# Where GpSimd forms the sums of the output weights: two batches, or one behind the last convolution of the first group

## The chip, the cores and the metric

The kernel runs on one core of a Trainium2 chip. The core has five engines that run at the same time, each with its own queue of instructions: TensorE (PE in the profile, with PEld for its weight loads), VectorE (DVE), ScalarE (ACT), GpSimd (POOL) and SyncE (SP), which here issues nearly all DMAs. An engine works through its queue in order; an instruction that waits for another engine holds up everything behind it. The metric is the device time of one execution in microseconds; the median of the runs is compared.

## The reference

The input is x, 16 sequences of 256 tokens of 512 features, all in float32. Three layers follow each other, each with a residual and a layer norm.

```python
x = _layernorm(x + _L0_attn_ref(x, ...), axis=-1)      # a state-space layer
x = _layernorm(x + _L0_xattn_ref(x, k, skip, ctx, ctx, 8), axis=-1)   # a long convolution
x = _layernorm(x + _L0_ffn_ref(x, ...), axis=-1)       # a linear layer with routed LoRA
```

The change lies in the first:

```python
xn = x * rsqrt(mean(x * x) + EPS) * w_norm
proj = einsum('bld,td->blt', xn, W_in)                 # z, xi, dt, Bm, Cm
xi = silu(causal depthwise conv of 4 taps(xi))
dt = softplus(dt + dt_bias);  dA = exp(-dt * exp(A_log))
u = (dt * mean of xi over a head)[..., None] * Bm
h = dA_t[..., None] * h + u_t;  y_t = sum(h * C_t)     # scan over the tokens
y = einsum('blh,ih->bli', y, W_h2i) * silu(z)
out = einsum('bli,di->bld', y, W_out) + residual
```

## The kernel before

The first layer runs in eight groups of 512 tokens (two sequences); the loop over g is at line 526. The second and third layers follow in another loop over eight slices and aren't touched.

**Products with seven instead of eight parts.** The projections and, in all groups but the last, the output product are formed with Strassen's scheme in Winograd's form: a product of two 2x2 block matrices from seven block products. The blocks' sums and differences must be made beforehand. For tokens these are `token_sums` (lines 221 to 226); for the projections' weights `weight_sums` (228 to 234), once, on GpSimd; for the output weights `w_o` it is `w_o_sums` (290 to 302), also once, on GpSimd, in the first group. With `w_o[r, j]` the four blocks, each of four tiles of 128x256, it makes T3 = w11 - w01 (line 295), T1 = w01 - w00 (298, in the place of w01), T2 = w11 - T1 (300) and T4 = w10 - T2 (301), sixteen instructions in all. T1 and T3 are read by the output products of the first group (`out_product`, line 740), T2 and T4 likewise.

**The order inside a group.** The scheduler is off: each engine's queue has the order in which the code calls its instructions. A loop over i (line 623) goes through ten projections; in the first group these are x0, x1, z0, x2, z1, x3, b0, c1, z2, z3. Each turn issues the first four block products of projection i, then the last three of projection i-1 (`finish_products`), the first sums of i (lines 344 to 347) and the last sums of i-1 (`finish_sums`, 356 to 359). When i-1 is an x, `finish_sums` also issues the convolution of two tiles of channels, `mixed` (552 to 566): on VectorE one scaling (559, or on ScalarE 557) and three multiply-and-adds (561) a tile. `mixes` collects the last of each tile. So the turn i = 4 holds the convolutions of tiles 4 and 5, and i = 6 those of tiles 6 and 7, the last of the group.

The tail of the group then runs on VectorE: `stepped` (583), `states` with one product (587) and two scans (590) for each of two halves ht, in turns i = 7 (ht 0) and i = 8 (ht 1), and `outputs` (595), one product a half. In turn i = 9 TensorE sums these over the states into `yps` (639), and ScalarE copies them to `yT` (662). After the loop `spread_heads` (698) multiplies by W_h2i, `gated` (712) gates z with the result, `out_sums` (731) makes the sums of the gated z, and the output products (740) use them with the sums of `w_o`.

**What GpSimd has in its queue in the first group.** `later` (489) puts `weight_sums` of later projections behind a convolution: `wait_for` adds a wait to the first of them for the last multiply-and-add issued so far, `mixes[-1]`. In turn i = 4 these are the sums of z2 and z3. `w_o_sums` is a generator with two parts. Its first part (T3) is issued in turn i = 4, directly behind them; its second part (T1, T2, T4) in turn i = 8, behind `rms(xs_next)`, whose last step `rstd` (375) is a GpSimd instruction.

**The next group's norm.** In turn i = 8 the squares of the next tokens are summed on ScalarE (371), VectorE makes the mean `ms` (373), GpSimd raises it to -1/2 (`rstd`, 375), and SP writes the result to a row in DRAM (`to_dram`, 394). After the loop SP loads the next tokens into `xnT` (217), which waits until TensorE has read the old ones, and reads the row back, spread over all partitions, as `rt` (398). VectorE then scales `xnT` by it (`normed`, 404). From `xnT` TensorE forms the dt product (418), and GpSimd the token sums (222 to 226).

Of the kernel before, what the change touches and what calls it, by code (L numbers as in the profile page):

```python
# [10 lines left out]
ALU = mybir.AluOpType  # L11
# [60 lines left out]
def decoder_kernel(  # L72
# [95 lines left out]
    def wait_for(ins, other):  # L168
        tc.add_manual_dep(
            ins.ins,  # L170
            other.ins.name,
            mybir.DependencyInfo(
                mybir.DependencyClass.Sync, mybir.DependencyReason.DATA
            ),
            reason="order",
        )
# [4 lines left out]
    with ExitStack() as s1:  # L181
# [89 lines left out]
        w_o = {}  # L271
# [15 lines left out]
        for k, name in enumerate(("T3", "T2", "T4")):  # L287
            w_o[name] = parts[k * HC : (k + 1) * HC]

        def w_o_sums():  # L290

            sub = nc.gpsimd.tensor_tensor
            w_o["T1"] = w_o[0, 1]
            for c in range(HC):
                sub(w_o["T3"][c], w_o[1, 1][c], w_o[0, 1][c], ALU.subtract)
            yield
            for c in range(HC):
                sub(w_o["T1"][c], w_o[0, 1][c], w_o[0, 0][c], ALU.subtract)
            for c in range(HC):
                sub(w_o["T2"][c], w_o[1, 1][c], w_o["T1"][c], ALU.subtract)  # L300
                sub(w_o["T4"][c], w_o[1, 0][c], w_o["T2"][c], ALU.subtract)
            yield

        xis = [p1.tile([P, GB, S + 3], F32, name=f"xi{i}") for i in range(4)]
        for t in xis:
# [25 lines left out]
        def first_products(w, p, third):  # L331

            al, be = [
                ps_s.tile([P, 512], F32, tag="s", name="s") if third else bank() for _ in range(2)
            ]
            product(al[:, 0:S], w, p, A11, "11", start=True)
            product(be[:, 0:S], w, p, S1, "T1", start=True)
            product(al[:, S:], w, p, S2, "T2", stop=True)
            product(be[:, S:], w, p, S3, "T3", stop=True)
            return al, be  # L340

        def first_sums(al, be, to):
            u = p2.tile([P, S], F32, tag="u", name="u", bufs=3)
            nc.scalar.copy(u, al[:, 0:S])
            nc.vector.tensor_tensor(u, u, al[:, S:], ALU.add)
            nc.vector.tensor_tensor(to[3], u, be[:, S:], ALU.add)
            nc.vector.tensor_tensor(to[3], to[3], be[:, 0:S], ALU.add)
            return u
# [146 lines left out]
        def with_identity(w):  # L495

            for k, blk in enumerate(BLOCKS_OUT):
                own = w[:, k, blk * P : (blk + 1) * P]
                if blk in SWAPPED_OUT:
                    for a, b in ((0, HP), (HP, 0)):  # L500
                        half = own[:, a : a + HP]
                        nc.vector.tensor_tensor(half, half, ident[:, b : b + HP], ALU.add)
                else:
                    nc.vector.tensor_tensor(own, own, ident, ALU.add)

        def centred(w, cols):

            ps = ps_t.tile([P, 512], F32, tag="tr", name="mw")
            for kc in range(KD):
                nc.tensor.matmul(  # L510
                    ps[:, 0:cols], share, w[:, kc, :], start=(kc == 0), stop=(kc == KD - 1)
                )
            for kc in range(KD):
                nc.vector.tensor_tensor(w[:, kc, :], w[:, kc, :], ps[:, 0:cols], ALU.subtract)
# [11 lines left out]
        for g in range(NG):  # L526
# [6 lines left out]
            accs, mixes, zs, zpairs, silus = [], [], [], [], []  # L533

            def places(kind, p):

                if kind == "x":
                    two = [t[:, :, 3:] for t in (xis[2 * p % 4], xis[2 * p % 4 + 1])]
                    return [t[:, b, :] for t in two for b in range(GB)]
                if kind == "z":  # L540
                    pair = gp.tile([P, 2, GT], F32, tag="zs", name="zs")
                    zpairs.append(pair)
                    two = [pair[:, e, :] for e in range(2)]
                    zs.extend(two)
                else:
                    two = [p2.tile([P, GT], F32, tag=kind, name=kind) for _ in range(2)]
                    (Bs if kind == "b" else Cs).extend(two)
                return [t[:, b * S : (b + 1) * S] for t in two for b in range(GB)]
# [19 lines left out]
            def head_means(ht):  # L568

                xm = ps_t.tile([P, GT], F32, tag="tr", name="xm")  # L570
                for q in range(4):
                    nc.tensor.matmul(  # L572
                        xm[32 * q : 32 * (q + 1), :],
                        mean.rearrange("p h n -> p (h n)"),
                        accs[4 * ht + q].rearrange("p b s -> p (b s)"),
                        start=True,
                        stop=True,
                    )
                return xm

            def stepped(xm, dtS):
                m = p2.tile([P, GT], F32, tag="acc", name="m", bufs=6)
                nc.vector.tensor_tensor(m, xm, dtS, ALU.mult)
                return m
# [19 lines left out]
            def finish_products():  # L604
                kind, p, al, be, u, to = before
                last_products(al, be, kinds[kind], p)
# [16 lines left out]
            for i, (kind, p) in enumerate(order):  # L623
                if g == 1 and i == 2:
                    with_identity(w_f)
                if g == 1 and i in (5, 6):
                    centred(*((w_f, D), (w_gl, NE + ER))[i - 5])
                if i == 6:
                    ms = [head_means(0)]
                al, be = first_products(kinds[kind], p, i % 3 == 0)  # L630
                if i == 8:
                    ms.append(head_means(1))
                if i == 9:


                    yps = ps_t.tile([P, S], F32, tag="tr", name="yps")
                    for ht in range(HT):
                        for b in range(GB):
                            nc.tensor.matmul(
                                yps[b * HP : (b + 1) * HP],  # L640
                                sel[:, ht].rearrange("p q h -> p (q h)"),
                                Bs[ht][:, b * S : (b + 1) * S],
                                start=(ht == 0),
                                stop=(ht == HT - 1),
                            )
                if before is not None:
                    finish_products()
                to = places(kind, p)
                u = first_sums(al, be, to)
                if i == 8:  # L650
                    states(1, stepped(ms[1], spreads[2]), spreads[3])
                if i == 6:
                    ms = [stepped(ms[0], spreads[0])]
                    spreads.append(spread(1, 1))
                if g == 0:
                    if i == 1:
                        parts = decays()
                    if i in (1, 2, 4):
                        next(parts)
                if i == 9:  # L660
                    yT = q3.tile([P, S], F32, tag="vn", name="yT", bufs=1)
                    nc.scalar.copy(yT, yps)
                if before is not None:
                    finish_sums((lambda: next(parts)) if g == 0 and i == 2 else None)
                if g == 0 and i == 3:
                    next(parts)
                if g == 0 and i in later:
                    for n, (w, k) in enumerate(later[i]):
                        ins = weight_sums(nc.gpsimd, w, k)
                        if n == 0:  # L670
                            wait_for(ins, mixes[-1])
                    if i == 4:
                        w_sums = w_o_sums()
                        next(w_sums)
                if i == 7:
                    states(0, ms[0], spreads[1])
                if i == 8:
                    outputs(0)
                    outputs(1)
                    if more:  # L680
                        rt = to_dram(rms(xs_next))
                    if g == 0:
                        next(w_sums)
                before = (kind, p, al, be, u, to)
                if i < 2 and late:
                    normalised(g - 1, late.pop(0))
                if i == 1 and more:
                    xs_next = load_x(g + 1)
# [180 lines left out]
    with ExitStack() as s2:  # L869
# [295 lines left out]
        for h in range(HX):  # L1165
# [38 lines left out]
            behind = None  # L1204
            if nxt:
                kv_n, T_n = kvs[0]
                cT_n, vT_next = cTs[0], vT_after
                behind = products(vT_next, cT_n, kv_n, 0)
# [196 lines left out]
```

## Time and profile before

| | us |
|---|---|
| median of three runs | 1437.86 |
| lowest and highest | 1437.38, 1440.82 |
| the profiled execution | 1436.66 |
| its span in the profile | 1434.8 |
| TensorE busy in the span | 1417.2 |
| VectorE busy | 1218.1 |
| GpSimd busy | 560.8 |

The lines of the profile read as follows. A line of a timeline gives the start and the length in us, the engine, the line of the code and the operation, the tile written and the tiles read, the shapes, and how many instructions are merged. What stands in brackets at its end is the time that the engine stood idle before it and what ended that. A line of the list of waits gives the engine and line that waited, what it waited for, the sum in us, how often, and the longest. The mean granted clock of TensorE over the span is 0.998.

### The profile page before, as it was taken

To read this page: it belongs to the slowest core of one execution; us is meant where nothing else is said; L and a number is where in the kernel's file an instruction comes from. 1 tells how busy PE (TensorE), PEld (TensorE's weight loads), DVE (VectorE), ACT (ScalarE), POOL (GpSimd) and SP (SyncE) were. 2 spreads that over 40 slices of the span, in tenths; PEclk is the share of its full clock that TensorE was granted. 3 is DMA by queue.
4 is the path that set the end of the run, shared out by engine and by line. 5 is a ranking of instruction groups with operands and counts; after the bars stand their busy time and mean duration, and the time that the engine had idled before them with its cause. 6 is when DMAs were issued, how large, how long until landed. Compare 5 with 4: busy or idle time off the path is not lost.

```text
span 1434.8 us, 19174 instructions
## 1 busy us (share of the span) xinstructions
PE 1417.2 (99%) x6972; PEld 916.4 (64%) x6972; DVE 1218.1 (85%) x2101; ACT 461.9 (32%) x964; POOL 560.8 (39%) x654
## 2 busy tenths in 40 slices
PE   9999999999999999999998999999999999999997
PEld 7878788888888888888884444444444444444443
DVE  6988778778888787877848999999999999999996
ACT  2422323233232332332311433333333343333331
POOL 5540010110100201001004776777677667766772
PEclk9999999999999999999999999999999999999999
DMA  8014021120121101212003122212221222122200
GB/s 299 33 37 131 8 72 56 38 83 8 44 77 45 62 29 38 83 43 89 16 16 115 55 67 80 75 61 69 74 81 61 69 74 82 59 70 74 81 29 23
DMA packets 50815, 93.38 MB, mean 65 GB/s; under 512 B 10656, under 2 KB 15008, under 8 KB 50720
## 3 DMA queue, kind: packets, MB, share of 16 engines
q1 hardware_dynamic: 50192, 92.15, 20.1%
q8 instruction: 55, 0.90, 0.3%
q14 instruction: 40, 0.33, 0.1%
q10 hardware_dynamic: 528, 0.00, 0.0%
HBM read 74.82 MB, written 17.32 MB: 64 GB/s over the span
## 4 chain that ended last, share of the span: by engine, by line
PE 93%; DVE 5%; issue 1%; ACT 1%; DMA 0%; POOL 0%; SPq 0%; POOLq 0%; DVEq 0%; ACTq 0%
PE mm L322 18%; PE y L981 15%; PE s L322 13%; PE y L999 12%; PE base L1160 8%; PE s L740 6%; PE mm L740 6%; PE yc L969 4%; PE gl L1227 2%; PE base L1156 2%; PE tr L1071 1%; DVE acc L561 1%; PE mm L698 1%; PE xm L572 1%; PE mm L827 1%
## 5 line engine op out<-in xcount | busy, mean ns | idle before, releaser
L1034 DVE TENSOR_TENSOR pr<-y,cT 128x1024 f32<-128x1024 f32 x126 | 148.4, 1220 | 41.6 <-PE y L999 37.2
L158 DVE TENSOR_TENSOR kv<-vT,cT 128x1024 f32<-128x1024 f32 x128 | 180.1, 1448 | 1.5 <-ACT vT L148 1.5
L999 PE MATMUL y<-kv 64*64 64x512 f32 x1408 | 179.6, 598 | 0.0
L561 DVE SCALAR_TENSOR_TENSOR acc<-xi,wc,acc 128x512 f32<-128x512 f32 x192 | 143.5, 761 | 7.4 <-ACT acc L557 1.8
L1044 DVE TENSOR_REDUCE red<-pr 128x128 f32<-128x1024 f32 x126 | 147.1, 1209 | 0.0
L981 PE MATMUL y<-kv 128*128 128x512 f32 x272 | 128.1, 594 | 4.0 <-DVE pr L1034 2.9
L999 PEld LDWEIGHTS y<-kv 64*64 64x64 f32 x1408 | 51.3, 132 | 119.1 <-issue 90.9
L917 POOL TENSOR_TENSOR o<-t,vT 64x384 f32<-64x384 f32 x64 | 121.2, 1894 | 4.4
L1160 PE MATMUL base<-w_f,ol 128*128 128x512 f32 x248 | 119.5, 605 | 0.0
L981 PE MATMUL y<-kv,Td 128*128 128x512 f32 x248 | 116.5, 592 | 0.0
L67 POOL TENSOR_TENSOR rs_a<-ve_a,nhalf 128x1 f32<-128x1 f32 x32 | 19.0, 594 | 243.7 <-DVE ve_a L65 243.7
L375 POOL TENSOR_TENSOR rstd<-ms,nhalf 128x4 f32<-128x4 f32 x8 | 8.1, 1018 | 259.0 <-DVE ms L373 259.0
L322 PE MATMUL mm<-XT,w_z 128*128 128x256 f32 x384 | 90.7, 379 | 0.0
L981 PEld LDWEIGHTS y<-kv,Td 128*128 128x128 f32 x248 | 47.1, 190 | 59.3 <-issue 59.1
L981 PEld LDWEIGHTS y<-kv 128*128 128x128 f32 x272 | 48.9, 190 | 55.5 <-issue 49.8
L946 POOL TENSOR_TENSOR xs<-kv 128x512 f32<-128x512 f32 x63 | 80.2, 1273 | 2.4
L322 PEld LDWEIGHTS mm<-XT,w_z 128*128 128x128 f32 x384 | 73.0, 190 | 9.9
L1160 PEld LDWEIGHTS base<-w_f,ol 128*128 128x128 f32 x248 | 42.3, 189 | 54.5 <-issue 54.5
L970 ACT COPY y<-yc 128x1024 f32<-128x1024 f32 x62 | 61.8, 997 | 33.9 <-PE yc L969 23.9
L1192 POOL TENSOR_TENSOR ol<-o,red 128x512 f32<-128x512 f32 x31 | 39.5, 1273 | 82.2 <-DVE red L1044 82.2
L322 PE MATMUL mm<-xnT,w_z 128*128 128x256 f32 x288 | 70.9, 382 | 0.0
L999 PE MATMUL y<-kvd,kv 64*64 64x512 f32 x128 | 65.2, 589 | 0.0
(278 smaller groups left out, 2950.0 us busy)
## 6 DMA issues: line engine op xcount, KB each, us to landing
cT<-in_ctxT SPq DMA_DIRECT2D x32, 448.0 KB
kv<-in_toep SPq DMA_DIRECT2D x32, 448.0 KB
xt<-in_x SPq DMA_DIRECT2D x32, 256.0 KB
xnT<-in_xT SPq DMA_DIRECT2D x8, 1024.0 KB
spread<-both SPq DMA_DIRECT2D x32, 256.0 KB
first<-xt SPq DMA_DIRECT2D x32, 256.0 KB
vn<-first SPq DMA_DIRECT2D x32, 256.0 KB
out<-res SPq DMA_DIRECT2D x31, 256.0 KB
```

The costliest lines, as they stand in the source:

```text
L158: last = nc.vector.tensor_tensor(kv[:, q, k * BQ : (k + NL // 2) * BQ], vT[:, q, blks].rearrange("p k (b i) -> p (k b) i", i=NH).unsqueeze ...
L322: nc.tensor.matmul(ps, w[:, p, a, kc, :], Xs[b][:, kc, :], start=start and kc == 0, stop=stop and kc == 1, skip_group_check=upon,)
L561: ins = nc.vector.scalar_tensor_tensor(acc, xi[:, :, k : k + S], wc[:, c, k : k + 1], acc, ALU.mult, ALU.add)
L740: nc.tensor.matmul(ps, own[a][c][:, n * P : (n + 1) * P], w_o[b][c], start=start and c == 0, stop=stop and c == HC - 1, skip_group_check=upon,
L917: nc.gpsimd.tensor_tensor(o[b : b + HP, :, 0:3], t[a : a + HP, :, 1:4], vT[a : a + HP, :, 1:4], ALU.add,)
L946: return nc.gpsimd.tensor_tensor(xs[:, q], moving(kv, q, 0), moving(kv, q, 1), ALU.add)
L970: nc.scalar.copy(y[1], yc.unsqueeze(1).to_broadcast([P, 2, BQ * NH * NH]))
L981: nc.tensor.matmul(bank_of(y, lb), w, moving(kv, q, mb), start=not late and lb not in begun, stop=False, skip_group_check=True,)
L999: return nc.tensor.matmul(bank_of(y, lb)[cols], T[rows, at, cols], src[rows], start=start, stop=False, skip_group_check=True,)
L1034: nc.vector.tensor_tensor(pr.rearrange("p (k b j) i -> p k b j i", k=2, j=NH), y[i].rearrange("p k (b j i) -> p k b j i", j=NH, i=NH), cT[ ...
L1044: nc.vector.tensor_reduce(red[:, q, 2 * i : 2 * i + 2, :].rearrange("p k t -> p (k t)"), pr, AX.X, ALU.add)
L1160: nc.tensor.matmul(base, o_l[:, kc, :], w_f[:, kc, :], start=(first and kc == kcs[0]), stop=False)
```

## The change

All sixteen sums are issued together in turn i = 6 of the first group, behind the calls that issue the convolutions of tiles 6 and 7, and the first of them gets a wait for the last multiply-and-add of tile 7. The generator becomes a plain function that takes the instruction to wait for. `rstd` (375), which stood between the two parts, comes after all sixteen in GpSimd's queue. The other engines' queues keep their order.

```diff
-        def w_o_sums():
+        def w_o_sums(behind):
 
             sub = nc.gpsimd.tensor_tensor
             w_o["T1"] = w_o[0, 1]
             for c in range(HC):
-                sub(w_o["T3"][c], w_o[1, 1][c], w_o[0, 1][c], ALU.subtract)
-            yield
+                ins = sub(w_o["T3"][c], w_o[1, 1][c], w_o[0, 1][c], ALU.subtract)
+                if c == 0:
+                    wait_for(ins, behind)
             for c in range(HC):
                 sub(w_o["T1"][c], w_o[0, 1][c], w_o[0, 0][c], ALU.subtract)
             for c in range(HC):
                 sub(w_o["T2"][c], w_o[1, 1][c], w_o["T1"][c], ALU.subtract)
                 sub(w_o["T4"][c], w_o[1, 0][c], w_o["T2"][c], ALU.subtract)
-            yield
...
                         if n == 0:
                             wait_for(ins, mixes[-1])
-                    if i == 4:
-                        w_sums = w_o_sums()
-                        next(w_sums)
+                if g == 0 and i == 6:
+                    w_o_sums(mixes[-1])
                 if i == 7:
                     states(0, ms[0], spreads[1])
                 if i == 8:
                     outputs(0)
                     outputs(1)
                     if more:
                         rt = to_dram(rms(xs_next))
-                    if g == 0:
-                        next(w_sums)
```

## The prediction

> **What bounds the kernel now.** I read four views in this order: the page's busy times and chain, the list of what TensorE waited for, the timeline of the first group of tokens set beside that of the second, and the issues of the SP queue.
>
> ```profile
> PE 1417.2 (99%) x6972; PEld 916.4 (64%) x6972; DVE 1218.1 (85%) x2101; ACT 461.9 (32%) x964; POOL 560.8 (39%) x654
> ...
> PE 93%; DVE 5%; issue 1%; ACT 1%; DMA 0%; POOL 0%; SPq 0%; POOLq 0%; DVEq 0%; ACTq 0%
> ```
>
> TensorE is busy for 99% of the span and carries 93% of the chain. So a change on GpSimd (POOL) counts only as far as it moves TensorE's few waits. Two of those waits lie in the first group, where the changed instructions run:
>
> ```profile
> PE yps L639 <- DVE b L595: 1.2, 1, 1.2
> ...
> PE s L740 <- DVE zs L359: 0.9, 1, 0.9
> ```
>
> Each occurs once in seven groups that run the same code. To see what the two cost, lay group 0 on group 1 in TensorE's timeline (start, length):
>
> ```profile
> 73.81 1.16 PE L639 MATMUL yps<-b,sel 128*64 128x256 f32 x8 [1.20 <-DVE b L595]
> ...
> 85.56 1.97 PE L740 MATMUL s<-w_o_sum,z_sum 128*128 128x256 f32 x8 [0.94 <-DVE zs L359]
> ```
> ```profile
> 171.61 1.08 PE L639 MATMUL yps<-b,sel 128*64 128x256 f32 x8
> ...
> 182.18 1.89 PE L740 MATMUL s<-w_o_sum,z_sum 128*128 128x256 f32 x8
> ```
>
> From the preceding L572 matmuls to yps it is 8.68 us in group 0 (65.13 to 73.81) and 7.24 in group 1 (164.37 to 171.61): 1.44 lost. From the first L740 matmuls to the second it is 2.93 (82.63 to 85.56) and 1.83 (180.35 to 182.18): 1.10 lost. With 0.2 in small pieces the stage loses 2.7 us, and no change of POOL's order can win more.
>
> The cause is VectorE (DVE), slow where POOL adds beside it:
>
> ```profile
> 58.17 4.31 POOL L295 TENSOR_TENSOR w_o_sum<-w_o 128x256 f32<-128x256 f32 x4
> 74.42 1.03 POOL L375 TENSOR_TENSOR rstd<-ms,nhalf 128x4 f32<-128x4 f32 x1 [11.94 <-DVE ms L373]
> 75.43 2.78 POOL L298 TENSOR_TENSOR w_o<-w_o 128x256 f32<-128x256 f32 x4
> ```
> ```profile
> 58.52 6.08 DVE L561 SCALAR_TENSOR_TENSOR acc<-xi,wc,acc 128x512 f32<-128x512 f32 x6
> ...
> 66.50 0.69 DVE L587 TENSOR_TENSOR b<-b,m 128x512 f32<-128x512 f32 x1
> 67.22 1.27 DVE L590 TENSOR_TENSOR_SCAN b<-spread,b 128x256 f32<-128x256 f32 x2
> ...
> 70.42 0.69 DVE L587 TENSOR_TENSOR b<-b,m 128x512 f32<-128x512 f32 x1
> 71.15 1.27 DVE L590 TENSOR_TENSOR_SCAN b<-spread,b 128x256 f32<-128x256 f32 x2
> ...
> 72.98 1.28 DVE L595 TENSOR_TENSOR b<-b,c 128x512 f32<-128x512 f32 x2
> ...
> 80.06 1.28 DVE L712 TENSOR_TENSOR zs<-zs,wh 128x512 f32<-128x512 f32 x2
> 81.25 3.51 DVE L731 TENSOR_TENSOR z_sum<-zs 128x256 f32<-128x256 f32 x4
> ...
> 156.17 4.56 DVE L561 SCALAR_TENSOR_TENSOR acc<-xi,wc,acc 128x512 f32<-128x512 f32 x6
> ...
> 178.97 1.43 DVE L731 TENSOR_TENSOR z_sum<-zs 128x256 f32<-128x256 f32 x4
> ```
>
> The six L561 take 6.08 beside L295 and 4.56 in group 1, where POOL rests. The four L731 take 3.51 beside L300/L301 and 1.43 in group 1. L712, which reads one operand from PSUM, takes its 1.28 beside POOL all the same. So the operations with two SBUF operands pay, those with a PSUM operand don't. Between 62.5 and 74.4 POOL is idle, and there DVE runs the tail of the group (L587, L590, L595) that yps waits for.
>
> **The change part by part.** The sums in one batch behind the last convolution: same 16 instructions, same work, new neighbours.
>
> 1. *L561 loses its neighbour.* POOL waits for the last of these L561, so they go at the row of group 1: 6.08 - 4.56 = 1.52 us earlier, ending at 63.0. All of it is on the path to yps: DVE has no gap from there to L595.
>
> 2. *The sums land on the tail.* POOL starts at about 63.07 (after its earlier wait for an L561, which ended at 52.34, it started at 52.42). Alone the 16 need 11.5 us: 2.75 for each four (L298), 1.50 for each of four L300/L301 pairs (78.16 to 79.66). So they last to 74.6 at least, over the whole tail. From 64.98 (L587, 1.52 earlier) to the first L595, seven instructions with two SBUF operands meet them: two L587, four L590, one L595. The price of one meeting: the four L561 beside the four L295 cost 1.52 / 4 = 0.38 each (128x512); the four L731 cost (3.51 - 1.43) / 4 = 0.52 each (128x256). No row shows a scan beside POOL. Bounds for L590: nothing (it might not share the port), or a whole POOL instruction, 0.73. I take 0.45, the middle of the two rows, since it too reads two SBUF operands, in pieces of 256. Sum: 3 x 0.38 + 4 x 0.45 = +2.9. Ends: +1.1 (scans free) and 7 x 0.73 = +5.1.
>    So the first L595 ends 2.9 - 1.5 = 1.4 later, and yps's wait grows from 1.2 to about 2.6. The second L595, which the second half of yps needs, meets POOL as well: 0.38, of which 0.3 shows, because the first half's matmuls cover only part of it.
>    The Trainium skill has a rule that speaks harder against this change ("SBUF — State Buffer", section on SBUF's two separate sides): the port pair that VectorE and GpSimd share is an exclusive lock, and the loser blocks for the whole of the other's instruction. The row above disagrees in size: a pair of L561 and L295 takes 1.13 us (58.52 to 59.66), not 0.75 + 0.73 = 1.48. By the rule the seven would cost the upper end and the total would be +3.0 instead of +0.5.
>
> 3. *L731 loses its neighbour.* With meetings POOL does one of its instructions per DVE instruction and is through at about 77, ahead of 81.25. L731 goes back to 1.43, 2.08 less. Only the part that TensorE waited for counts: 1.10, plus 0.08 for the following matmuls (1.97 against 1.89): -1.2. DVE keeps the rest as lead.
>
> 4. *rstd moves behind the sums.* On POOL, L375 was at 74.42, ahead of twelve sums; now all sixteen stand before it, and it runs at about 77. Behind it are the row's DMA and, in SP's order, the load of xnT and the read of the row back as rt:
>
> ```profile
> 75.48 0.39 SPq L394 DMA_DIRECT2D row<-rstd  x1
> 80.79 0.40 SPq L217 DMA_DIRECT2D xnT<-in_xT  x1
> 84.94 0.34 SPq L398 DMA_DIRECT2D rt<-row  x1
> ```
>
>    The row is issued at about 78.1, still ahead of L217's own wait for TensorE, so xnT isn't held up. L398 waits for the row to land, 9.5 us after its issue here, 8.0 in group 1 (171.59 to 179.61): now at 86.1 to 87.6 instead of 84.94. rt landed at 91.6 and DVE reached its use (L404) at 91.94, so there is no slack on DVE's side: DVE would be ready at 91.94 + 1.7 - 2.1 = 91.5, rt lands at 92.8 to 94.3 by the old 6.7 us, and DVE waits 1.3 to 2.8. Behind L404 on DVE stands L767. TensorE next needs the result at the dt product L418, 97.82 before and 98.3 now; L404 ends 2.74 after it starts, at 95.5 to 97.0. POOL's token sums (95.38 to 100.5) are needed only at 109.3. So I cost this step at nothing, with 1.3 us of cover left at worst; every us beyond it goes on the time.
>
> Sum: (2.9 - 1.5) + 0.3 - 1.2 = **+0.5 us**. The profiled execution took 1436.66 us (span 1434.8 and 1.9 around it) and becomes 1437.2; the median of the runs shown, 1437.86, is 1.2 above that execution, so the median becomes **1438.4**. Ends: the whole 2.7 won, and +3.0 for whole-instruction blocking (5.1 - 1.5 + 0.6 - 1.2).
>
> **The rivals.**
>
> A. *It does what it looks like.* If scans and POOL don't meet, step 2 is +1.1, yps waits 0.4 less than before, and the total is -0.4 + 0.3 - 1.2 = -1.3: 1436.6; with cheaper L587 and L595 too, down to -2.7: 1435.2. For it: no row shows a scan beside POOL. Against: everything with two SBUF operands that does stand beside POOL pays.
>
> B. *rt comes late.* If POOL ends at 78.5 and the row takes 9.8 us, the longest here (263.55 to 273.38), rt is issued at about 89.4 and lands at 96.1, or at 97.3 by group 1's 7.9 us. L404 then ends at up to 100.0 and holds L418 for up to 1.7: total +2.2, 1440.1. Against: with xnT mostly loaded by then, rt should land faster than it did beside it.
>
> C. *TensorE's gap grows past what its clock stands; this one ends slower.* Place: before yps. With a whole POOL instruction per meeting the gap is 1.2 + 3.6 = 4.8 us, and the total +3.0 without more. If the granted clock then falls, the 8.8 us of matmuls from yps to L740 stretch, by up to 8.8 at half speed. From 1.3 us lost there the change is slower by over 0.3%; total +3.0 to +11.8, 1440.9 to 1449.7. Against: the granted clock is 1.00 in every stretch of this group, gaps of 1.2 and 0.9 included, and the expected gap is 2.6. The Trainium skill ("TensorE: Matmul & The Clock Gate", rules for kernel authors) asks for no gaps over some 3 us, as the clock is halved after them; an estimate from its 3.4 us window is 1.7 us lost; no run here shows it.
>
> **How the numbers follow.** About 0.3%, 4.3 us, is what a measurement of this kernel can tell from no change. Forecast 0.55, A 0.22, B 0.09, C 0.07, anything I don't see 0.07. Forecast, A and B lie within 0.3% but for the scatter of the runs (1437.38 to 1440.82). C ends slower with most of its chance; the unseen I put mainly on the slower side, since the best case is capped at 2.7. So faster 0.03, same 0.87, slower 0.10. The range takes in A down to its end and B, and leaves out most of C: 1434.8 to 1442.0.
>
> **What would show it.** Right: L561 in group 0 at 4.6; L590 beside the sums at 1.9 to 2.3 a pair; yps waiting 2 to 3 us; no wait at the L740 matmuls; L731 at 1.43; L375 at about 77; a short idle of DVE before L404. Wrong: L590 at 1.27 beside POOL (A), TensorE idle before L418 (B), a granted clock under 1 after yps (C).

## The result, and the profile after

The changed kernel takes 1440.50 us in the median of 22 runs (1439.28 to 1441.43), the kernel before 1437.78 in 22 runs (1436.19 to 1440.82). The ratio is 1.0019, with a 95% interval of 1.0013 to 1.0025: 2.7 us slower, a small loss that is clear of the scatter of the runs. The profiled execution took 1440.3 us, its span is 1438.5.

The page's busy times and chain are those of before, within 2 us:

```profile
PE 1419.2 (99%) x6972; PEld 916.9 (64%) x6972; DVE 1217.5 (85%) x2101; ACT 461.3 (32%) x964; POOL 562.0 (39%) x654
...
PE 93%; DVE 5%; issue 1%; ACT 1%; DMA 0%; POOL 0%; SPq 0%; POOLq 0%; DVEq 0%; ACTq 0%
```

In the list of TensorE's waits, the one at the L740 matmuls is gone, and that before yps has grown from 1.2 us to 3.2, in two pieces:

```profile
PE yps L639 <- DVE b L595: 3.2, 2, 2.8
```

TensorE's timeline in group 0 shows both, and one thing more (T1 now stands at line 299, T2 and T4 at 301 and 302, and the lines of the code behind 680 have moved up by three, so L740 is now L737, L731 is L728 and L712 is L709):

```profile
75.11 0.65 PE L639 MATMUL yps<-b,sel 128*64 128x256 f32 x4 [2.79 <-DVE b L595]
76.15 0.85 PE L639 MATMUL yps<-b,sel 128*64 128x256 f32 x4 [0.39 <-DVE b L595]
76.92 3.44 PE L322 MATMUL mm<-xnT,w_z 128*128 128x256 f32 x8
...
87.93 1.89 PE L737 MATMUL s<-w_o_sum,z_sum 128*128 128x256 f32 x8
```

The eight L322 matmuls behind yps took 1.99 us before and take 3.44 now. Their line in the kernel before:

```profile
74.90 1.99 PE L322 MATMUL mm<-xnT,w_z 128*128 128x256 f32 x8
```

Their shape and data are the same; TensorE's clock isn't. In the table by stretches the number before the last two is the granted clock, here in steps of one us from 74.6 on:

```profile
74.60:75.60 1.00, 0.49 (x4) 0.23 (x4) 1.00 (x2) 0.00 (x0) 1.00 (x2) 1.00 0.00 0
75.60:76.60 1.00, 0.61 (x6) 0.20 (x4) 1.00 (x2) 0.00 (x0) 1.00 (x1) 0.94 0.00 0
76.60:77.60 1.00, 1.00 (x4) 0.59 (x3) 0.86 (x4) 0.37 (x1) 0.92 (x3) 0.50 0.00 0
77.60:78.60 1.00, 1.00 (x4) 0.82 (x3) 0.41 (x1) 0.00 (x0) 0.88 (x1) 0.50 0.00 0
78.60:79.60 1.00, 1.00 (x3) 0.78 (x3) 0.00 (x0) 0.38 (x1) 0.00 (x0) 0.50 0.12 1
79.60:80.60 1.00, 1.00 (x5) 0.88 (x4) 0.00 (x0) 0.00 (x0) 0.00 (x0) 0.85 0.13 1
```

The clock is at half for 3.4 us: the missing shares, 0.06 + 3 x 0.50 + 0.15, make 1.7 us of TensorE's time, of which 1.45 fall on the L322 matmuls (their starts 76.92 to 80.20 against 74.90 to 76.73). In the kernel before the clock was 1.00 in these stretches.

VectorE's and GpSimd's timelines over the same time:

```profile
58.39 4.56 DVE L561 SCALAR_TENSOR_TENSOR acc<-xi,wc,acc 128x512 f32<-128x512 f32 x6
...
64.84 0.84 DVE L587 TENSOR_TENSOR b<-b,m 128x512 f32<-128x512 f32 x1
65.71 2.17 DVE L590 TENSOR_TENSOR_SCAN b<-spread,b 128x256 f32<-128x256 f32 x2
...
69.80 1.21 DVE L587 TENSOR_TENSOR b<-b,m 128x512 f32<-128x512 f32 x1
71.05 2.17 DVE L590 TENSOR_TENSOR_SCAN b<-spread,b 128x256 f32<-128x256 f32 x2
...
73.78 2.32 DVE L595 TENSOR_TENSOR b<-b,c 128x512 f32<-128x512 f32 x2
76.02 0.69 DVE L373 TENSOR_SCALAR ms<-ss 128x4 f32<-128x4 f32 x1
...
83.52 1.28 DVE L709 TENSOR_TENSOR zs<-zs,wh 128x512 f32<-128x512 f32 x2
84.72 1.42 DVE L728 TENSOR_TENSOR z_sum<-zs 128x256 f32<-128x256 f32 x4
...
95.25 2.74 DVE L404 SCALAR_TENSOR_TENSOR xnT<-xnT,wn,rt 128x512 f32<-128x512 f32 x4 [1.84 <-DMA rt<-row]
```
```profile
63.03 3.23 POOL L295 TENSOR_TENSOR w_o_sum<-w_o 128x256 f32<-128x256 f32 x4 [4.96 <-DVE acc L561]
66.23 3.55 POOL L299 TENSOR_TENSOR w_o<-w_o 128x256 f32<-128x256 f32 x4
...
77.44 1.04 POOL L375 TENSOR_TENSOR rstd<-ms,nhalf 128x4 f32<-128x4 f32 x1
```

L561 and the S3 sums (L728) have lost their neighbour and run at the lengths of the other groups. The tail pays instead: two scans take 2.17 us where they took 1.27. An instruction with a single SBUF operand can pay too: the mean `ms` (L373) takes 0.69 us beside a sum, where it took 0.16 in the kernel before with GpSimd idle. It stands behind L595, so yps doesn't wait for it. The row and its reading back on SP's queue have moved as well; DVE waits 1.84 us for rt, and TensorE doesn't wait for DVE there:

```profile
78.51 0.39 SPq L394 DMA_DIRECT2D row<-rstd  x1
84.26 0.40 SPq L217 DMA_DIRECT2D xnT<-in_xT  x1
88.51 0.34 SPq L398 DMA_DIRECT2D rt<-row  x1
```

Laid on the kernel before from the L572 matmuls (65.13 and 65.01) to the first matmuls of group 1 (109.30 and 111.58), group 0 is 46.57 us instead of 44.17, 2.4 more: +1.42 to yps, +0.72 from yps to L322, +1.45 for the slow matmuls, -1.10 for the lost wait at L740 and -0.08 behind it.

The two profiled executions differ by 3.6 us, though, more than the medians. The rest lies in a place that the change doesn't touch, the first slice of the second stage. TensorE's timeline there, before and after:

```profile
771.53 1.13 PE L981 MATMUL y<-kv 128*128 128x512 f32 x2 [1.74 <-DVE pr L1034]
773.75 1.12 PE L981 MATMUL y<-kv 128*128 128x512 f32 x2 [1.09 <-ACT y L970]
774.71 1.88 PE L981 MATMUL y<-kv,Td 128*128 128x512 f32 x4
```
```profile
773.81 1.13 PE L978 MATMUL y<-kv 128*128 128x512 f32 x2 [1.73 <-DVE pr L1031]
776.02 1.93 PE L978 MATMUL y<-kv 128*128 128x512 f32 x2 [1.09 <-ACT y L967]
777.75 2.82 PE L978 MATMUL y<-kv,Td 128*128 128x512 f32 x4
```

The waits are the same, 1.7 and 1.1 us with one matmul between. But in the second execution the clock fell behind them: 2.82 us for matmuls of 1.88, 1.7 us in all up to 785.95 (781.98 before). So a single pair of profiles can't tell what the change does to this place. The experiments had to.

### The profile page after: what moved, and what is told of

It is laid out like the page before. It is cut to its first block, busy times and chain, and to the rows that moved or that the text cites. A ratio compares the mean times of both kernels' runs of the same rounds, so it can differ in the third digit from the quotient of the medians.

```text
span 1438.5 us, 19174 instructions
## 1 busy us (share of the span) xinstructions
PE 1419.2 (99%) x6972; PEld 916.9 (64%) x6972; DVE 1217.5 (85%) x2101; ACT 461.3 (32%) x964; POOL 562.0 (39%) x654
## 4 chain that ended last, share of the span: by engine, by line
PE 93%; DVE 5%; issue 1%; ACT 1%; DMA 0%; POOL 0%; SPq 0%; POOLq 0%; DVEq 0%; ACTq 0%
PE mm L322 18%; PE y L978 15%; PE s L322 13%; PE y L996 12%; PE base L1157 8%; PE s L737 6%; PE mm L737 6%; PE yc L966 4%; PE gl L1224 2%; PE base L1153 2%; PE tr L1068 1%; PE mm L695 1%; DVE acc L561 1%; PE xm L572 1%; PE mm L824 1%
## 5 line engine op out<-in xcount | busy, mean ns | idle before, releaser
L561 DVE SCALAR_TENSOR_TENSOR acc<-xi,wc,acc 128x512 f32<-128x512 f32 x192 | 141.9, 753 | 7.4 <-ACT acc L557 1.7
L322 PE MATMUL mm<-XT,w_z 128*128 128x256 f32 x384 | 90.7, 379 | 0.0
L322 PEld LDWEIGHTS mm<-XT,w_z 128*128 128x128 f32 x384 | 73.0, 190 | 9.9
L322 PE MATMUL mm<-xnT,w_z 128*128 128x256 f32 x288 | 72.4, 388 | 0.0
```

What stands on the lines that cost most here:

```text
L322: nc.tensor.matmul(ps, w[:, p, a, kc, :], Xs[b][:, kc, :], start=start and kc == 0, stop=stop and kc == 1, skip_group_check=upon,)
L561: ins = nc.vector.scalar_tensor_tensor(acc, xi[:, :, k : k + S], wc[:, c, k : k + 1], acc, ALU.mult, ALU.add)
```

## The experiments

The theory: (1) a VectorE instruction with two SBUF operands that meets a GpSimd sum takes 0.4 to 0.5 us longer, one fed from PSUM doesn't; (2) the wait of TensorE that follows is followed by a fall of its clock, which costs as much again; (3) the second stage has a gap of its own behind which the clock falls in some executions, whatever the kernel. The rivals: that the slow matmuls have another cause, that the loss comes from rstd and the row, or that each half of the change loses by itself.

Each kernel ran 8 to 11 times beside the kernel before on the same chip; the first four ran on one chip, the next four on a second, the last two on a third. Medians in us:

| kernel | median | lowest to highest | ratio to before, 95% interval |
|---|---|---|---|
| T3 alone moved | 1436.63 | 1435.20 to 1438.48 | 0.9993 [0.9984, 1.0002] |
| the twelve others alone moved | 1441.81 | 1440.19 to 1442.58 | 1.0026 [1.0016, 1.0037] |
| the change, gap before yps filled | 1439.17 | 1437.17 to 1441.04 | 1.0007 [0.9998, 1.0016] |
| the sums spread over PSUM-fed stretches | 1435.40 | 1433.55 to 1436.92 | 0.9985 [0.9977, 0.9994] |
| before, gap of the second stage filled | 1437.30 | 1436.38 to 1438.00 | 0.9995 [0.9986, 1.0004] |
| the change, gap of the second stage filled | 1439.77 | 1438.30 to 1440.40 | 1.0012 [1.0003, 1.0021] |
| the change, both gaps filled | 1438.28 | 1437.55 to 1438.65 | 1.0000 [0.9991, 1.0009] |
| spread, gap of the second stage filled | 1434.25 | 1433.81 to 1434.90 | 0.9972 [0.9962, 0.9982] |
| both filled, but only 3 matmuls before yps | 1438.49 | 1437.49 to 1440.66 | 1.0009 [1.0000, 1.0018] |
| both filled, but only 6 matmuls before yps | 1438.56 | 1437.41 to 1439.06 | 1.0007 [0.9998, 1.0016] |

The kernel before had 1438.03 beside the first four (30 runs), 1437.87 beside the next four (30 runs) and 1436.83 beside the last two (21 runs).

**One half of the change: T3 alone behind the last convolution.**

```diff
-                    if i == 4:
-                        w_sums = w_o_sums()
-                        next(w_sums)
+                if g == 0 and i == 6:
+                    w_sums = w_o_sums(mixes[-1])
+                    next(w_sums)
```

> Of the change only its first half is made: the four T3 sums stand behind the last convolution, the twelve others stay behind rstd. Theory (each two-SBUF DVE instruction that meets a POOL sum pays 0.4 to 0.5 us, and a wait of TensorE of nearly 3 us before yps costs a fall of its clock on top): L561 in group 0 at 4.6, T3 meets one L587 and one L590, +0.6 in all, so the wait before yps falls from 1.2 to about 0.3, the clock stays at 1.00 there, and the wait of the L740 matmuls for L359 stays at 0.9 because L731 still meets the later sums. About 1.0 us under before: 1436.8. Rival (the loss comes from the second half alone being moved or from rstd and the row): also faster than before, but with yps's wait unchanged at 1.2.

Measured: 1436.63. The timelines of this kernel's TensorE and VectorE in group 0:

```profile
73.00 1.16 PE L641 MATMUL yps<-b,sel 128*64 128x256 f32 x8 [0.42 <-DVE b L597]
```
```profile
66.00 1.69 DVE L592 TENSOR_TENSOR_SCAN b<-spread,b 128x256 f32<-128x256 f32 x2
70.34 1.27 DVE L592 TENSOR_TENSOR_SCAN b<-spread,b 128x256 f32<-128x256 f32 x2
```

The wait before yps is 0.42 instead of 1.2. The first pair of scans, one of which meets T3, takes 1.69, the second pair, with GpSimd idle, 1.27. So this half gains where it was expected to, and the loss isn't in it. The gain of 1.4 in the medians isn't clear of the runs' scatter, as the interval shows.

**The other half alone: T1, T2 and T4 behind the last convolution.**

```diff
             for c in range(HC):
-                sub(w_o["T1"][c], w_o[0, 1][c], w_o[0, 0][c], ALU.subtract)
+                ins = sub(w_o["T1"][c], w_o[0, 1][c], w_o[0, 0][c], ALU.subtract)
+                if c == 0:
+                    wait_for(ins, behind[0])
...
+                if g == 0 and i == 6:
+                    w_behind.append(mixes[-1])
+                    next(w_sums)
...
-                    if g == 0:
-                        next(w_sums)
```

> The other half alone: T3 stays where it was, beside the last convolution, and the twelve sums T1, T2, T4 go behind it, ahead of rstd. Theory: L561 stays at 6.1, the tail meets the twelve sums for +2.5, yps waits 3.5 to 4 us, no wait at the L740 matmuls (-1.2), and the granted clock falls behind yps for 1.5 us or more: 2.5 - 1.2 + 1.5 = +2.8, 1440.6. Rival (no clock effect, only waits): +1.3, 1439.1.

Measured: 1441.81, 3.8 over before. TensorE's timeline:

```profile
75.90 2.16 PE L641 MATMUL yps<-b,sel 128*64 128x256 f32 x8 [3.20 <-DVE b L597]
```

The wait is 3.20, a little under the expected 3.5 to 4, and yps itself already runs at the lower clock (2.16 us instead of 1.16). The clock in the stretches from 75.6 on is 0.64, 0.50, 0.50, 0.66: again 3.4 us at half. The time is 2.7 over what waits alone would make, 1439.1, and 1.2 over what was expected with the fall; a wait of 0.79 in group 1 (131.77), which the profiled execution of the kernel before doesn't have, and the scatter of the second stage can be part of that. So the whole loss comes with the twelve sums that stand beside the tail. The row is late in this kernel too, but TensorE doesn't wait at the dt product, so the row isn't what costs the time.

**The gap before yps filled.** Twelve matmuls of the identity, which yps overwrites, keep TensorE busy through most of the wait, in group 0 only. The profile has two records for each of them.

```diff
                     yps = ps_t.tile([P, S], F32, tag="tr", name="yps")
+                    for _ in range(12 if g == 0 else 0):
+                        nc.tensor.matmul(yps[:, 0:P], ident, ident, start=True, stop=True)
```

> The changed kernel with twelve extra 128x128 matmuls of the identity in TensorE's queue ahead of yps in group 0 only, about 2.6 us that fill the wait; yps overwrites what they write. Theory (the fall of the granted clock comes from the gap): clock 1.00 from 75 to 80, the eight L322 matmuls behind yps back from 3.44 to 1.99, yps still starts at about 75.1: 1.45 us under the changed kernel, 1439.0, unless a clock fall elsewhere moves. Rival (the slow matmuls have another cause, as memory traffic of POOL or DVE): they stay at 3.4 and the time at 1440.5.

Measured: 1439.17. TensorE's timeline:

```profile
72.45 2.84 PE L638 MATMUL yps<-ident 128*128 128x128 f32 x24
75.37 0.65 PE L641 MATMUL yps<-b,sel 128*64 128x256 f32 x4
...
77.08 1.99 PE L322 MATMUL mm<-xnT,w_z 128*128 128x256 f32 x8
```

VectorE and GpSimd do the same beside each other as in the changed kernel, yps starts as late as there (0.26 later, as this execution was 0.3 later from the start), and the L322 matmuls are back at 1.99. So it was the gap and nothing that runs beside TensorE. These kernels were meant to show only group 0, and they still scatter by 2.4 to 3.9 us each. In the profiled execution of this one (1439.19) the clock falls in the second stage as well: the matmuls of 1.88 us take 2.55 there. That called for a second set.

**All sums where VectorE reads PSUM.** Two T3 behind the last L561, two behind the scans of the first half, T1 and T2 behind rstd, T4 behind the S3 sums.

```diff
+                if g == 0 and i == 6:
+                    w_o_sums("T3", 0, 2, mixes[-1])
                 if i == 7:
-                    states(0, ms[0], spreads[1])
+                    scanned = states(0, ms[0], spreads[1])
+                    if g == 0:
+                        w_o_sums("T3", 2, HC, scanned)
                 if i == 8:
...
                     if g == 0:
-                        next(w_sums)
+                        w_o_sums("T1", 0, HC)
+                        w_o_sums("T2", 0, HC)
...
-                out_sums("S3", acc_tiles(), (0, 0), (1, 0), ALU.subtract)
+                ins = out_sums("S3", acc_tiles(), (0, 0), (1, 0), ALU.subtract)
+                if g == 0:
+                    w_o_sums("T4", 0, HC, ins)
```

> All sums placed where VectorE reads PSUM: two T3 behind the last L561, two T3 behind the scans of ht 0, then rstd, T1 and T2, and the four T4 behind the S3 sums (L731). Theory (only two-SBUF instructions pay): L561 at 4.6, L587, L590, L595 and L731 at their lengths without POOL, yps waits 0.1 or less, no wait at the L740 matmuls: -2.5 against before, 1435.3, clock 1.00 in group 0. Rival (any DVE instruction beside POOL pays, or each added wait costs its own time): the PSUM-fed sums grow and the gain is under 1.5 us.

Measured: 1435.40, faster than both kernels, with an interval that lies under 1. TensorE's and VectorE's timelines:

```profile
72.51 1.08 PE L641 MATMUL yps<-b,sel 128*64 128x256 f32 x8
```
```profile
65.83 1.27 DVE L591 TENSOR_TENSOR_SCAN b<-spread,b 128x256 f32<-128x256 f32 x2
...
79.87 1.43 DVE L735 TENSOR_TENSOR z_sum<-zs 128x256 f32<-128x256 f32 x4
```

No wait before yps, none at the L740 matmuls, and every two-operand instruction of the tail at the length it has without GpSimd. The sixteen sums are the same; where they stand is worth 5 us between this kernel and the changed one.

The profiled execution (1436.63) is one of the slower ones of this kernel. In the second stage it has the same two waits as the others, 1.74 and 1.09 us, and behind them a longer fall:

```profile
771.19 2.08 PE L988 MATMUL y<-kv 128*128 128x512 f32 x2 [1.09 <-ACT y L977]
773.06 3.62 PE L988 MATMUL y<-kv,Td 128*128 128x512 f32 x4
```

The granted clock in steps of two us from 770 on is 0.53, 0.50, 0.50 and 0.76: the missing shares make 2 x (0.47 + 0.50 + 0.50 + 0.24) = 3.4 us, which is 6.8 us at half speed, twice the fall of the changed kernel. The stage is 2.8 us longer by it (13.25 from 768.98 to 782.23, against 10.45 in the kernel before, from 771.53 to 781.98). So the same two waits are followed by no fall, by one of 1.7 us or by one of 2.8. That fits runs of the kernel before near 1436.5, 1438.3 and above 1439; of these only one of the lowest was profiled.

**The second stage's gap filled, in four kernels.** Seven matmuls of the identity into a bank that isn't in use yet, ahead of the second half of the first slice:

```diff
+            if h == 0:
+                fill = ps_b.tile([P, D], F32, tag="base", name="base")
+                for _ in range(7):
+                    nc.tensor.matmul(fill[:, 0:P], ident, ident, start=True, stop=True)
             if nxt:
                 convolve(y, kv, T, Td, kvd, 1)
```

The kernel before with it:

> The kernel before with seven extra 128x128 matmuls of the identity that fill TensorE's wait of 1.7 us in the first slice of the second stage (ahead of the first matmul of its second half). Theory (the runs of every kernel fall into two clusters some 1.9 us apart because the granted clock falls behind that wait in some executions and not in others): the upper cluster goes, median 1436.5, nearly all runs within 1436.0 to 1437.5. Rival (the scatter comes from elsewhere): median 1438.0 and the same spread, or later by what the matmuls cost.

Measured: 1437.30, between 1436.38 and 1438.00; beside it the kernel before ran between 1436.18 and 1440.73. TensorE's timeline shows the gap closed and the matmuls behind it at their full speed:

```profile
770.53 1.72 PE L1246 MATMUL base<-ident 128*128 128x128 f32 x14
772.42 1.12 PE L981 MATMUL y<-kv 128*128 128x512 f32 x2 [0.17 <-DVE pr L1034]
```

The upper executions went, as expected, and the spread fell from 4.5 to 1.6 us. The median is 0.8 over the 1436.5 that was expected; why the lower executions rose isn't settled. In the profiled one a wait of 0.74 in group 1 (129.18) is there, which the profiled execution of the kernel before doesn't have; whether the other runs have it isn't known.

The changed kernel with it:

> The changed kernel with the same fill in the second stage. Theory: what is left against the filled kernel before is the first group alone: +0.8 of waits and +1.45 of the fall of the clock behind yps, so about 2.3 above it: 1438.8. Rival (the change also makes the fall of the second stage likelier, or the group costs less): a difference of under 1.5 or over 3 us.

Measured: 1439.77, 2.5 over the filled kernel before; the theory said 2.3. TensorE's timeline in group 0 shows the fall, which set in a little earlier here:

```profile
75.25 2.16 PE L639 MATMUL yps<-b,sel 128*64 128x256 f32 x8 [2.81 <-DVE b L595]
77.34 2.50 PE L322 MATMUL mm<-xnT,w_z 128*128 128x256 f32 x8
```

The changed kernel with both gaps filled:

> The changed kernel with both fills, that ahead of yps in group 0 and that in the second stage. Theory: no fall of the clock in either place; what is left against the filled kernel before is the sum of waits alone, +0.8 and 0.2 or so for the fill that overruns: 1437.3 to 1437.6. Rival (the fall behind yps costs nothing by itself): equal to the changed kernel with the second fill alone.

Measured: 1438.28, within 1.1 us. That is 1.5 under the kernel with the second fill alone: the price of the fall behind yps, freed from the second stage. And it is 1.0 over the filled kernel before: the price of the waits. Not all of these lie before yps. In the profiled execution the row comes back late enough to hold up TensorE at the dt product:

```profile
96.34 3.76 DVE L404 SCALAR_TENSOR_TENSOR xnT<-xnT,wn,rt 128x512 f32<-128x512 f32 x4 [4.06 <-DMA rt<-row]
```
```profile
100.15 0.43 PE L418 MATMUL d_lg<-xnT,w_dt 128*32 128x128 f32 x8 [0.31 <-DVE xnT L404]
```

VectorE waits 4.06 us for rt, and L404 takes 3.76 instead of 2.74, now that it stands beside GpSimd's token sums (from 97.89 on). The dt product takes 0.5 longer by it (1.53 from L418 to the next matmuls, 1.01 in the filled kernel before). In the changed kernel itself TensorE reaches L418 later, behind the fall of the clock, and doesn't wait there in either of its two profiles. The level is 0.7 above what was expected, as in the filled kernel before.

The spread sums with it:

> The sums spread over VectorE's PSUM-fed stretches, with the fill in the second stage. Theory: both gains add, 2.5 under the filled kernel before: 1434.0, nearly all runs within 1.2 us. Rival: 1435.4 as without the fill.

Measured: 1434.25, within 1.1 us, 3.1 under the filled kernel before and 0.28% under the kernel before itself (interval 0.18% to 0.38%). This is the fastest kernel of the study. The difference of 3.1 is more than the 2.5 that was expected and than the 2.7 that the first group could lose; the wait in group 1, 0.74 in the profiled execution of the filled kernel before and 0.25 here, may be the rest, which isn't tested.

**How large a gap may be.** Two kernels with both fills, but fewer matmuls ahead of yps, leave part of that gap open:

> The changed kernel with the fill in the second stage and three matmuls instead of twelve ahead of yps: TensorE's idle time there goes from 2.8 to about 2.1 us, plus 0.4 between the halves of yps. Theory (the clock falls by how much of some 3.4 us was idle, wherever that stretch begins): the fall comes in part of the executions only; the times lie between 1438.3 (both fills) and 1439.8 (none ahead of yps), spread over both. Rival (any wait of 2 us or more costs the whole fall): 1439.8.

> The same with six matmuls: idle time before yps about 1.4 us, as long as in the kernel before (1.2). Theory: no fall there, 1438.3 as with twelve, spread about 1 us. Rival (a gap of 1.4 and one of 0.4 shortly behind it suffice, as 1.7 and 1.1 do in the second stage in some executions): median of 1438.8 or more with a spread of 2 us.

TensorE's timelines of the two:

```profile
75.37 0.65 PE L641 MATMUL yps<-b,sel 128*64 128x256 f32 x4 [2.06 <-DVE b L595]
```
```profile
75.09 0.65 PE L641 MATMUL yps<-b,sel 128*64 128x256 f32 x4 [1.40 <-DVE b L595]
```

With 2.06 us open the times run from 1437.49 to 1440.66 (median 1438.49): most executions lie where the filled kernel does, and four of eleven 0.9 us and more above its median, with a mean clock over the span of 0.996 or 0.997, which is 0.998 or 0.999 in the filled kernel. So at 2.1 us a fall seems to come in a part of the executions, as expected; that is argued from the mean clock alone, since the one that was profiled (1437.74) has no fall. With 1.40 open the median is 1438.56 and five of eleven still have a mean clock of 0.997. That lies between what theory (1438.3) and rival (1438.8) said, and it stays open whether a gap of 1.4 us here is safe. Both comparisons with the filled kernel also go across chips: the kernel with both gaps filled ran on the second, these two on the third, where the median of the kernel before is 1.0 lower. And with six matmuls the late row shows as well: in the profiled execution TensorE waits 0.25 at the dt product.

## Why the prediction was right or wrong

The measured 1440.50 lies in the range of 1434.8 to 1442.0, and the change is within 0.3%, as the likeliest outcome said. The central 1438.4 was 2.1 too low, and the sign was not called: +0.5 was forecast, +2.7 came. That the value lies in the range is partly luck: the upper part of the range stood there for rival B and was to leave out most of rival C, and what came is the fall of the clock that only C had.

- **Step 1** (L561 from 6.08 to 4.56): exact.
- **Step 2** (the sums on the tail): right in mechanism and size. Seven meetings were to cost 2.9. Measured beside before: 0.15 and 0.52 for the two L587, 0.90 for each pair of L590 (the 0.45 that was assumed for a scan without any row), 0.52 for each L595: 3.0. yps was to be 1.4 late and is 1.42 late; its second half was to wait 0.3 and waits 0.39.
- **The lock rule** of the Trainium skill ("SBUF — State Buffer", the section on SBUF's two separate sides) gave 5.1 for these seven, whole-instruction blocking. The rows say 3.0: that instructions with two SBUF operands pay is as the page has it, the price of one meeting isn't.
- **Step 3** (L731 and the wait at L740): -1.2 forecast, -1.10 and -0.08 measured.
- **Step 4** (rstd and the row): rstd at about 77, measured 77.44; DVE waiting 1.3 to 2.8 us for rt, measured 1.84; TensorE not waiting at L418, and it doesn't. Rival B, with its price of 1.7 at L418, did not happen in the changed kernel. But the cover was thinner than was said: with both gaps filled VectorE waits 4.06 us for rt where 2.8 was the worst, L404 takes 3.76 where 2.74 was taken, and 0.5 us shows at L418. Of the four profiles without a fall behind yps, two show such a wait.
- **Rival A** is out: the scans do meet the sums.
- **The step that failed is the missing term: the clock behind the gap.** The sum counted the gap before yps as a wait only. The fall of the clock was named, as rival C, but tied to a gap of 4.8 us from whole-instruction blocking, and "the expected gap is 2.6" stood there as the evidence against it. The gap came out at 2.79, and the clock fell for 3.4 us: +1.45 on the L322 matmuls, and some 0.3 of the 0.72 between yps and L322. The two filled kernels put the fall at 1.5. With it the sum is 1.4 + 0.3 - 1.2 + 1.5 to 1.8 = 2.0 to 2.3, of the measured 2.4 in this group. The rule of the page "TensorE: Matmul & The Clock Gate" of the Trainium skill (the table in the section on why this matters for your kernels: no gaps over some 3 us) was read as a threshold that 2.6 stays under; here 2.79 was already enough. The estimate of 1.7 for a fall, which the prediction worked out from that page's window, was right for this place. A term like that should have been given its price at 2.6 already, with a chance, instead of none.
- **The evidence against rival C**, "the granted clock is 1.00 in every stretch of this group, gaps of 1.2 and 0.9 included", came from one execution and from gaps half as long. Of the thirty runs of the kernel before beside the first four experiments, 12 lie between 1436.1 and 1436.7 and 13 between 1437.9 and 1438.7. Beside the next four the groups are less sharp, but there too the upper runs go when the gap of the second stage is filled; in the execution that was profiled the clock happened to stay at 1.00 there. The scatter of 3.4 us over the three runs shown was taken as noise, and it held a hint of this.

## What to carry to other kernels

When an idle engine's work is moved, it gets new neighbours: price each VectorE instruction that it will then stand beside, and put GpSimd's work where VectorE reads PSUM, which costs nothing here. On a kernel bound by TensorE, a gap has two prices, the wait itself and the matmuls behind it at half clock. Here every profiled gap of 2.8 us or more was followed by a fall, and so were two gaps of 1.7 and 1.1 us close together in three of six profiles: count both prices from the first size on, and the second with a chance below it. If runs of one kernel fall into groups, look for such a gap before comparing medians, and fill it in both kernels.

## What the runs showed of the hardware

- The clock fell behind a gap of 2.79 us before yps (2.81 in the other profile of the changed kernel that leaves the gap open, 3.20 with the twelve sums moved). In the second stage it fell behind 1.73 and 1.09 us, with one matmul of 1.1 between, in three of the six profiles that leave these waits open. Gaps of 1.20 and 0.94, of 2.06 and 0.48, and of 1.40 and 0.48 left it at 1.00 in the profiles here.
- Behind yps a fall lasted 3.4 us at half speed for two sizes of the gap: the missing shares add to 1.7 us in the changed kernel (gap 2.79) and 0.36 + 0.50 + 0.50 + 0.34 = 1.7 in the one with the twelve sums moved (gap 3.20). It can last twice as long: 6.8 us at half speed in the second stage of the profiled execution of the spread sums, behind the same waits as elsewhere.
- A scan (L590, 128x256) that meets a GpSimd sum of the same shape goes from 0.63 to 1.08 us. PSUM-fed multiplies don't pay: in the kernel before L712 takes 1.29 and 1.28 beside the sums L300 and L301, and 1.28 in group 1 with GpSimd idle. A second SBUF operand isn't needed to pay: L373, with one, goes from 0.16 to 0.69.
- The row of 2 KB that is written in four-byte pieces takes 8 to 10.5 us from its issue until the DMA that reads it is issued (75.48 to 84.94 before, 78.51 to 88.51 after, 78.11 to 88.64 with the twelve sums moved, 171.59 to 179.61 in group 1 before).
